# The experts' scatter adds its rows inside the transfer instead of gathering and adding them first

## The chip, the cores and the metric

The kernel runs on one core of a Trainium2 chip. The metric is the device time of one execution in microseconds (us), lower is better. TensorE (PE) does the matrix products, its weight loads are a row of their own (PEld), VectorE (DVE) and ScalarE (ACT) do the elementwise work, GpSimd (POOL) does small elementwise work and issues every indirect transfer, that is every transfer whose rows are picked by a list of indices. SyncE (SP) issues plain transfers. All transfers run on the core's 16 DMA engines.

## The reference

The block takes `x` of 4 x 2048 tokens with 256 features. A linear attention layer is added to it, then a mixture of experts. The second half is what matters here:

```
h = _layernorm(x) * (1 + cb) + sb                       # x: after attention
logits = h @ w_router.T ; gates = softmax ; top 2 of 8 experts
keep   = place of the token in its expert < capacity    # capacity 1280
topk_gates = topk_gates * keep / (sum + 1e-6)
hidden = silu(h @ w_gate.T)                             # 256 -> 512, shared
y      = sum over experts e: combine[:, e] * (hidden @ w_down[e].T)
x      = x + gb * y
```

A token goes to two experts, so a row of the output receives up to two additions, from two different experts; within one expert a token stands once at most.

## The kernel before, in words

The first stage runs over 16 groups of 512 tokens: attention, router, and the place of each token in its experts' lists. It writes the rows after attention to the output in DRAM (`out`, line 779). With an indirect transfer from POOL (line 641) it also writes one row of 1036 numbers per kept (token, expert) pair to a table of slots in DRAM, 1280 slots per expert: the normalised token, its scale, shift and gate vectors, its eight combine weights and its token number.

The second stage runs over the 8 experts, one after another (`expert`, line 667). An expert has 1280 slots, that is ten tiles of 128 rows. They are worked in three blocks of 4, 4 and 2 tiles (`BLOCKS`); a tile is called by its place j in its block. For each block:

- SP loads the slot rows (`rows`, line 661; four buffers in all, loaded one expert ahead). DVE casts the token numbers to integers (`tok`, line 672) and applies scale and shift (`hm`, lines 688 and 689).
- PE turns `hm` over (line 694), ACT copies it out (`hT`, line 695), PE multiplies by the gate weights (`ph`, line 700), ACT and DVE make the SiLU (`th`, line 708, and `hid`, line 709).
- PE multiplies by the expert's own weights into PSUM (`pe`, line 714; two buffers), eight matmuls per tile. DVE evacuates each tile with the combine weight and the gate into `y` (line 721). The `y` tile holds a block of four tiles and has two buffers, so the first evacuation of a block may start only when the transfers that read the block two before have landed.

The addition to the output takes three steps. At the head of an expert, POOL gathers the output's rows of its ten tiles into `xc` (line 675), ten indirect transfers. DVE adds them (line 725) behind each evacuation. POOL writes the sums back (line 726, called a put below), ten indirect transfers. The same row may have been written by an earlier expert. Therefore every gather waits until all puts of the expert before have landed (`after(got, added)`). `xc` has two buffers by the parity of the expert. In the program the first put of an expert also waits until its gathers have landed.

The instructions of one engine run in the order in which they stand in its queue. In the second stage that order is set by a scheduler that works from the dependencies, not written out by hand. POOL's queue in this stage holds nothing but gathers and puts: ten gathers of expert e, then its ten puts, then the ten gathers of expert e + 1. DVE's queue mixes evacuations, additions, `hid`, `tok` and `hm`, the last two of the next expert's blocks.

Of the kernel before, what the change touches and what calls it, by code (L numbers as in the profile page):

```python
# [36 lines left out]
F32 = mybir.dt.float32  # L37
AF = mybir.ActivationFunctionType
ALU = mybir.AluOpType
AX = mybir.AxisListType  # L40

P = 128
NB, L, D = 4, 2048, 256
# [3 lines left out]
N = NB * L  # L47
# [14 lines left out]
TPE = CAP // P  # L62
# [4 lines left out]
def adaln_block(ctx: ExitStack, tc, x, wqkvT, woutT, wrT, wgT, wdT, cT, wmod, out):  # L67
    nc = tc.nc
# [7 lines left out]
    def bank(name):  # L76
        return ps.tile([P, 512], F32, tag="bank", name=name)
# [5 lines left out]
    def load_x(g):  # L83
# [17 lines left out]
        out=hsel, in_=hsel, compare_op=ALU.is_ge, fill=0.0, base=0,  # L101
# [3 lines left out]
        out=hsel, in_=hsel, compare_op=ALU.is_ge, fill=0.0, base=DH - 1,  # L105
# [3 lines left out]
    for q in range(2):  # L109
# [4 lines left out]
        out=tri8, in_=tri8, compare_op=ALU.is_gt, fill=0.0, base=0,  # L114
# [8 lines left out]
    for j in range(NT):  # L123
        for s in (1, -1):
            nc.gpsimd.affine_select(
                out=spread[:, j], in_=spread[:, j], compare_op=ALU.is_ge, fill=0.0, base=-32 * j * s,
# [111 lines left out]
    def after(later, earlier):  # L238

        for e in earlier:  # L240
            tc.add_manual_dep(
                later.ins, e.ins.name, mybir.DependencyInfo(mybir.DependencyClass.Sync, mybir.DependencyReason.DATA),
                reason="rows in DRAM",
            )

    def apart(inst, group, join=True):

        tc.declare_no_dep(inst.ins, group=group, query=mybir.DependencyQuery.ANY_SYNC, reason="different rows")
        if join:
            tc.add_to_no_dep_group(group, inst.ins)  # L250
# [258 lines left out]
    to_slots, added = [], []  # L509
# [144 lines left out]
    def load_rows(e):  # L654
        wds[e] = e3.tile([P, NF, D], F32, tag="wd", name=f"wd_{e}", bufs=3)
        nc.scalar.dma_start(wds[e], wdT[:, e * D : (e + 1) * D].rearrange("(f p) d -> p f d", p=P))
        rows[e] = []
        for i, n in BLOCKS:
            r = e3.tile([P, 4, W], F32, tag="rows", name=f"rows_{e}_{i}")
            at = e * CAP + i * P  # L660
            load = nc.sync.dma_start(
                r[:, :n, :], slots[at : at + n * P, :].rearrange("(j p) w -> p j w", p=P)
            )
            after(load, to_slots)
            rows[e].append(r)

    def expert(e):
        xc = xcs[e % 2]
        toks = []
        for (i, n), r in zip(BLOCKS, rows[e]):  # L670
            tok = e6.tile([P, 4], I32, tag="tok", name=f"tok_{e}_{i}")
            nc.vector.tensor_copy(tok[:, :n], r[:, :n, O_TOK])
            toks.append(tok)
            for j in range(n):
                got = nc.gpsimd.indirect_dma_start(  # L675
                    out=xc[:, i + j, :],
                    out_offset=None,
                    in_=out[:, :],
                    in_offset=bass.IndirectOffsetOnAxis(ap=tok[:, j : j + 1], axis=0),
                    bounds_check=N - 1,  # L680
                    oob_is_err=False,
                )
                after(got, added)
        added.clear()
        for (i, n), r, tok in zip(BLOCKS, rows.pop(e), toks):
            m = n * P
            hm = e2.tile([P, 4, D], F32, tag="hm", name=f"hm_{e}_{i}")
            nc.vector.tensor_tensor(hm[:, :n], r[:, :n, :D], r[:, :n, O_CB : O_CB + D], ALU.mult)
            nc.vector.tensor_tensor(hm[:, :n], hm[:, :n], r[:, :n, O_SB : O_SB + D], ALU.add)
            hT = e2.tile([P, NH, G], F32, tag="hT", name=f"hTe_{e}_{i}")  # L690
            for h in range(NH):
                pt = bank(f"pte_{e}_{i}_{h}")
                for j in range(n):
                    nc.tensor.transpose(pt[:, j * P : (j + 1) * P], hm[:, j, h * P : (h + 1) * P], ident)  # L694
                nc.scalar.copy(hT[:, h, :m], pt[:, :m])  # L695
            hid = e2.tile([P, NF, G], F32, tag="hid", name=f"hid_{e}_{i}")
            for f in range(NF):
                ph = mbank(f"ph_{e}_{i}_{f}")
                for k in range(NH):
                    nc.tensor.matmul(  # L700
                        ph[:, :m],
                        wg_sb[:, k, f * P : (f + 1) * P],
                        hT[:, k, :m],
                        start=(k == 0),
                        stop=(k == NH - 1),
                    )
                th = e2.tile([P, G], F32, tag="th", name=f"th_{e}_{i}_{f}")
                nc.scalar.activation(th[:, :m], ph[:, :m], AF.Tanh, scale=0.5)  # L708
                nc.vector.scalar_tensor_tensor(hid[:, f, :m], th[:, :m], 1.0, ph[:, :m], ALU.add, ALU.mult)  # L709
            pe = ps_e.tile([P, 4, D], F32, tag="psc", name=f"pe_{e}_{i}")  # L710
            y = e2.tile([P, 4, D], F32, tag="y", name=f"y_{e}_{i}")
            for j in range(n):
                for f in range(NF):
                    nc.tensor.matmul(  # L714
                        pe[:, j, :],
                        hid[:, f, j * P : (j + 1) * P],
                        wds[e][:, f, :],
                        start=(f == 0),
                        stop=(f == NF - 1),
                    )  # L720
                nc.vector.scalar_tensor_tensor(  # L721
                    y[:, j, :], pe[:, j, :], r[:, j, O_CW + e : O_CW + e + 1], r[:, j, O_GB : O_GB + D],
                    ALU.mult, ALU.mult,
                )
                nc.vector.tensor_tensor(y[:, j, :], y[:, j, :], xc[:, i + j, :], ALU.add)  # L725
                put = nc.gpsimd.indirect_dma_start(  # L726
                    out=out[:, :],
                    out_offset=bass.IndirectOffsetOnAxis(ap=tok[:, j : j + 1], axis=0),
                    in_=y[:, j, :],
                    in_offset=None,  # L730
                    bounds_check=N - 1,
                    oob_is_err=False,
                )
                apart(put, f"expert_{e}")
                added.append(put)

# [3 lines left out]
    with tc.manual_schedule(engines={ET.PE, ET.Activation, ET.DVE, ET.Pool}):  # L740
# [26 lines left out]
        for s in range((NG + 2) * NT):  # L767
            g, j = divmod(s, NT)
# [85 lines left out]
    def mbank(name):  # L854
        return ps_m.tile([P, 512], F32, tag="mbank", name=name)

    e2 = ctx.enter_context(tc.tile_pool(name="e2", bufs=2))
    e3 = ctx.enter_context(tc.tile_pool(name="e3", bufs=4))
    e6 = ctx.enter_context(tc.tile_pool(name="e6", bufs=6))
    xcs = []  # L860
    for i in range(2):
        xc = e2.tile([P, TPE, D], F32, tag=f"xc{i}", name=f"xc{i}", bufs=1)
        nc.vector.memset(xc, 0.0)
        xcs.append(xc)
    load_rows(0)
    for e in range(NE):
        if e + 1 < NE:
            load_rows(e + 1)
        expert(e)
# [31 lines left out]
```

## Time and profile before

| | us |
|---|---|
| median of 4 runs (1050.0 to 1059.29) | 1053.91 |
| the profiled execution, its own time | 1063.31 |
| its span in the trace | 1061.6 |
| slot rows of the last group begin to be sent (POOL) | 694.4 |
| first PE work of the experts' stage | 716.2 |
| last put issued (POOL) | 1053.5 |

| engine | busy over the span | share |
|---|---|---|
| PE | 901.4 | 85% |
| DVE | 639.8 | 60% |
| POOL | 566.6 | 53% |
| ACT | 439.9 | 41% |

The profile is of one execution. An engine's busy time is the time of its instructions; "idle before" a line is time in which it stood before that instruction, and the arrow names what came last before it could start. "Landing" of a transfer is the time from its issue to its completion. The granted clock of PE is 1.00 at full speed.

The two groups of indirect transfers that the change touches have 80 instructions each: gathers 84.9 us of POOL's time (1061 ns each on the mean), puts 83.9 us (1049 ns). The 80 additions on DVE take 424 ns each at the median.

### The profile page before, as it was taken

Reading aid. Unit: us, or ns where it says so; the run is one execution under the profiler, and the core shown is the slowest. Engines: PE = TensorE matmul, PEld = TensorE weight load, DVE = VectorE, ACT = ScalarE, POOL = GpSimd, SP = SyncE. Lnnn points to the kernel's source line nnn. Section 1 sums busy time; section 2 is a strip of 40 time slices with the busy share of each in tenths; the row PEclk is TensorE's granted clock in tenths of the full one; section 3 lists DMA queues with packets and bytes.
Section 4 is the critical chain, followed back from the end, with each engine's and each line's share of the span. In section 5 each row is a group of like instructions: output and inputs, shape, how many; then the busy total and the mean of one; then the engine's idle time right before and its main releaser. Section 6 shows DMA issues by size and latency. Waiting matters only on the chain. (4 is left out here: it accounts for less than half of the span.)

```text
span 1061.6 us, 18137 instructions
## 1 busy us (share of the span) xinstructions
PE 901.4 (85%) x6832; PEld 638.0 (60%) x6832; DVE 639.8 (60%) x1244; ACT 439.9 (41%) x1054; POOL 566.6 (53%) x738
## 2 busy tenths in 40 slices
PE   5659998699989999898999988409999898898996
PEld 5437666466656666766666666305676665666664
DVE  3326666558767876876787687435565454454543
ACT  0456665366556656655665533202212212122221
POOL 3023526456667665766756766635355454544653
PEclk9879999799999999999999999659999999999998
DMA  5088988642343344223312111336646645556431
GB/s 198 3 318 325 386 312 294 227 182 104 118 181 128 114 181 181 106 81 124 129 46 89 48 37 45 88 144 240 221 164 211 227 172 194 194 183 226 155 110 55
DMA packets 71096, 173.61 MB, mean 164 GB/s; under 512 B 13664, under 2 KB 34400, under 8 KB 71008
## 3 DMA queue, kind: packets, MB, share of 16 engines
q1 hardware_dynamic: 39040, 101.66, 26.6%
q0 software_dynamic: 26112, 63.45, 16.2%
q10 hardware_dynamic: 5856, 7.35, 2.1%
q8 instruction: 53, 0.87, 0.3%
q14 instruction: 35, 0.29, 0.1%
HBM read 68.66 MB, written 129.20 MB: 186 GB/s over the span
## 5 line engine op out<-in xcount | busy, mean ns | idle before, releaser
L714 PE MATMUL pe<-wd,hid 128*128 128x256 f32 x640 | 164.5, 397 | 21.5 <-DVE y L721 19.5
L436 DVE TENSOR_TENSOR at<-psc,tri 128x1024 f32<-128x1024 f32 x128 | 150.1, 1214 | 22.9 <-PE psc L430 22.9
L641 POOL DMA_INDIRECT slots<-hrow,idx x128 | 130.0, 1016 | 62.2 <-issue 35.3
L714 PEld LDWEIGHTS pe<-wd,hid 128*128 128x128 f32 x640 | 120.2, 195 | 70.8 <-DVE y L721 40.9
L700 PE MATMUL ph<-hTe,wg_sb 128*128 128x512 f32 (+1 forms) x384 | 155.8, 532 | 0.0
L726 POOL DMA_INDIRECT out_dram<-y,tok x80 | 83.9, 1049 | 109.9 <-DVE y L725 60.6
L708 ACT ACTIVATE th<-ph 128x512 f32<-128x512 f32 (+1 forms) x96 | 50.5, 526 | 197.4 <-PE ph L700 192.1
L675 POOL DMA_INDIRECT xc<-out_dram,tok x80 | 84.9, 1061 | 71.4 <-issue 42.9
L700 PEld LDWEIGHTS ph<-hTe,wg_sb 128*128 128x128 f32 x384 | 71.7, 194 | 41.7 <-issue 31.4
L721 DVE SCALAR_TENSOR_TENSOR y<-pe,rows 128x256 f32<-128x256 f32 x80 | 38.6, 483 | 92.8 <-PE pe L714 74.2
L709 DVE SCALAR_TENSOR_TENSOR hid<-th,ph 128x512 f32<-128x512 f32 (+1 forms) x96 | 57.2, 596 | 50.8 <-ACT th L708 50.8
L504 PE MATMUL pw<-wob,oT 128*128 128x256 f32 x256 | 70.7, 400 | 18.1 <-ACT kk L371 14.4
L461 POOL TENSOR_TENSOR s_acc<-s_acc,s_add 128x256 f32<-128x256 f32 x56 | 40.7, 726 | 76.7 <-ACT s_add L460 69.3
L430 PE MATMUL psc<-qeo,k 32*128 32x256 f32 x1024 | 74.2, 404 | 2.2 <-DVE at L436 2.1
L338 DVE SCALAR_TENSOR_TENSOR k<-exk,k 128x512 f32<-128x512 f32 x32 | 23.6, 738 | 85.6 <-ACT k L337 85.6
L504 PEld LDWEIGHTS pw<-wob,oT 128*128 128x128 f32 x256 | 46.6, 193 | 41.0 <-issue 16.6
L483 PE MATMUL po<-at,vpad 128*32 128x128 f32 x2048 | 69.9, 278 | 0.0
L332 PE MATMUL pk<-hTa,wqkv_sb 128*128 128x512 f32 x128 | 63.6, 623 | 4.4 <-ACT k L337 4.4
L332 PE MATMUL pq<-hTa,wqkv_sb 128*128 128x512 f32 x128 | 61.3, 604 | 5.1 <-ACT q L337 5.1
L483 PEld LDWEIGHTS po<-at,vpad 128*32 128x32 f32 x2048 | 52.6, 110 | 21.4 <-issue 21.2
L346 PE MATMUL pv<-wqkv_sb,hTa 128*128 128x256 f32 x256 | 61.9, 397 | 3.6 <-ACT pos L589 3.6
L695 ACT COPY hTe<-pte 128x512 f32<-128x512 f32 (+1 forms) x48 | 24.2, 516 | 86.2 <-PE pte L694 86.0
(153 smaller groups left out, 1667.4 us busy)
## 6 DMA issues: line engine op xcount, KB each, us to landing
slots<-free SPq DMA_DIRECT2D x80, 518.0 KB, 6.9
rows<-slots SPq DMA_DIRECT2D x16, 2072.0 KB, 8.6
rows<-slots SPq DMA_DIRECT2D x8, 1036.0 KB, 5.6
x<-in_x_dram SPq DMA_DIRECT2D x16, 512.0 KB, 4.1
out_dram<-x SPq DMA_DIRECT2D x16, 512.0 KB, 3.2
wd<-in_wdT_dram ACTq DMA_DIRECT2D x8, 512.0 KB, 3.7
slots<-hrow,idx POOLq DMA_INDIRECT x128, 3.4
wmod_sb<-in_wmod_dram ACTq DMA_DIRECT2D x1, 1536.0 KB, 8.7
```

What stands on the lines that cost most here:

```text
L332: nc.tensor.matmul(pq, wqkv_sb[:, k, o + h * P : o + (h + 1) * P], hT[:, k, :], start=(k == 0), stop=(k == NH - 1))
L346: nc.tensor.matmul(pv[:, i * D : (i + 1) * D], hT[:, k, (j + i) * P : (j + i + 1) * P], wqkv_sb[:, k, 2 * D : 3 * D], start=(k == 0), stop ...
L430: nc.tensor.matmul(psc[:, a, h], kT[r : r + 32, h, cols], qeo[r : r + 32, h, :, cols], start=True, stop=True,)
L436: masked = nc.vector.tensor_tensor(at, psc[:, 2 * m : 2 * m + 2].rearrange("p i h q t -> p (i h q) t"), tri.unsqueeze(1).to_broadcast([P, ...
L483: nc.tensor.matmul(po[32 * a : 32 * a + 32, h * P : (h + 1) * P], vp[:, j, h * 4 + a, q : q + 2, :], att[a // 2][:, a % 2, h, q, :], start ...
L504: nc.tensor.matmul(pw[:, :D], oT[:, h, :], wob[:, h, :], start=(h == 0), stop=(h == NH - 1))
L641: row = nc.gpsimd.indirect_dma_start(out=slots[:, :], out_offset=bass.IndirectOffsetOnAxis(ap=idx[:, c, j : j + 1], axis=0), in_=hr[:, j, ...
L675: got = nc.gpsimd.indirect_dma_start(out=xc[:, i + j, :], out_offset=None, in_=out[:, :], in_offset=bass.IndirectOffsetOnAxis(ap=tok[:, j ...
L700: nc.tensor.matmul(ph[:, :m], wg_sb[:, k, f * P : (f + 1) * P], hT[:, k, :m], start=(k == 0), stop=(k == NH - 1),)
L709: nc.vector.scalar_tensor_tensor(hid[:, f, :m], th[:, :m], 1.0, ph[:, :m], ALU.add, ALU.mult)
L714: nc.tensor.matmul(pe[:, j, :], hid[:, f, j * P : (j + 1) * P], wds[e][:, f, :], start=(f == 0), stop=(f == NF - 1),)
L726: put = nc.gpsimd.indirect_dma_start(out=out[:, :], out_offset=bass.IndirectOffsetOnAxis(ap=tok[:, j : j + 1], axis=0), in_=y[:, j, :], in ...
```

## The change

The gathers and the additions go. The put carries an addition (`compute_op=ALU.add`), so that the transfer adds `y` to what stands in the output's row. The wait moves with it: every put of an expert now waits until all puts of the expert before have landed (`prior`). The two `xc` buffers and their clearing go as well. In the changed kernel the put stands on line 715, the evacuation on 711, the product into `pe` on 704.

```diff
     def expert(e):
-        xc = xcs[e % 2]
         toks = []
         for (i, n), r in zip(BLOCKS, rows[e]):
             tok = e6.tile([P, 4], I32, tag="tok", name=f"tok_{e}_{i}")
             nc.vector.tensor_copy(tok[:, :n], r[:, :n, O_TOK])
             toks.append(tok)
-            for j in range(n):
-                got = nc.gpsimd.indirect_dma_start(
-                    out=xc[:, i + j, :],
-                    out_offset=None,
-                    in_=out[:, :],
-                    in_offset=bass.IndirectOffsetOnAxis(ap=tok[:, j : j + 1], axis=0),
-                    bounds_check=N - 1,
-                    oob_is_err=False,
-                )
-                after(got, added)
+        prior = list(added)
         added.clear()
...
-                nc.vector.tensor_tensor(y[:, j, :], y[:, j, :], xc[:, i + j, :], ALU.add)
                 put = nc.gpsimd.indirect_dma_start(
                     out=out[:, :],
                     out_offset=bass.IndirectOffsetOnAxis(ap=tok[:, j : j + 1], axis=0),
...
                     oob_is_err=False,
+                    compute_op=ALU.add,
                 )
+                after(put, prior)
                 apart(put, f"expert_{e}")
                 added.append(put)
...
-    xcs = []
-    for i in range(2):
-        xc = e2.tile([P, TPE, D], F32, tag=f"xc{i}", name=f"xc{i}", bufs=1)
-        nc.vector.memset(xc, 0.0)
-        xcs.append(xc)
     load_rows(0)
```

## The prediction, made before the changed kernel had run

> **What bounds the kernel now.** The groups of instructions come first. The change touches 80 gathers (L675), 80 puts (L726) and 80 additions on DVE. What it can give is limited by the engine that sets the stage's length, so the line of that engine is to be read beside them:
>
> ```profile
> L714 PE MATMUL pe<-wd,hid 128*128 128x256 f32 x640 | 164.5, 397 | 21.5 <-DVE y L721 19.5
> L726 POOL DMA_INDIRECT out_dram<-y,tok x80 | 83.9, 1049 | 109.9 <-DVE y L725 60.6
> L675 POOL DMA_INDIRECT xc<-out_dram,tok x80 | 84.9, 1061 | 71.4 <-issue 42.9
> ```
>
> POOL is free half of the time in this stage, and the time it spends on gathers costs nothing by itself. PE, however, sat idle 19.5 us until an evacuation (L721) had been done. Next I cut the experts' stage at each expert's last evacuation and read PE there. Columns: stretch, its length, busy PE, PEld, DVE, ACT, POOL, then the granted clock, the share of the DMA engines, GB/s.
>
> ```profile
> 757.50:799.00 41.50, 39.35 (x149) 26.61 (x148) 21.86 (x41) 9.29 (x18) 20.29 (x20) 0.96 0.59 206
> 799.00:842.70 43.70, 39.59 (x149) 26.73 (x148) 21.67 (x42) 9.20 (x18) 21.95 (x20) 0.96 0.57 197
> 842.70:886.90 44.20, 39.90 (x150) 26.84 (x150) 21.61 (x41) 9.20 (x18) 21.66 (x20) 0.96 0.56 192
> 886.90:931.00 44.10, 39.59 (x149) 26.91 (x148) 21.71 (x41) 9.20 (x18) 20.97 (x20) 0.96 0.56 192
> 931.00:972.70 41.70, 38.38 (x151) 26.19 (x150) 21.68 (x41) 9.20 (x18) 20.98 (x20) 0.99 0.57 200
> 972.70:1015.80 43.10, 40.77 (x153) 27.46 (x152) 21.72 (x41) 9.89 (x19) 21.38 (x20) 0.96 0.54 184
> ```
>
> Six experts take 258.3 us. PE is busy 237.6 of them and idle 20.7. One expert is 38.4 us of PE work where the clock is nearly full (fifth row), the others take 39.4 to 40.8 us for the same matmuls at a lower clock. PE is the bound. What can be won is its idle time and the time that its clock loses behind it: at most 258.3 - 6 x 38.4 = 27.9 us. DVE (21.7 of 43 us) and POOL (21) are far from being bounds.
>
> Who causes the idle time, from the waits in the experts' stage (us in total, times, longest):
>
> ```profile
> DVE y L721 <- DMA out_dram<-y,tok: 18.6, 4, 5.0
> DVE tok L672 <- DMA rows<-slots: 16.4, 14, 3.7
> DVE y L725 <- DMA xc<-out_dram,tok: 2.6, 1, 2.6
> ```
>
> Four times an evacuation waited for puts to land, and once an addition waited for its gather. The timeline of expert 3 shows one of the four:
>
> ```profile
> 871.82 1.04 POOL L726 DMA_INDIRECT out_dram<-y,tok  x1 [6.15 <-DVE hid L709]
> ...
> 876.25 0.98 POOL L726 DMA_INDIRECT out_dram<-y,tok  x1 [0.31 <-issue]
> ...
> 882.89 0.48 DVE L721 SCALAR_TENSOR_TENSOR y<-pe,rows 128x256 f32<-128x256 f32 x1 [4.72 <-DMA out_dram<-y,tok]
> ...
> 883.43 3.44 PE L714 MATMUL pe<-wd,hid 128*128 128x256 f32 x8 [3.75 <-DVE y L721]
> ```
>
> The chain behind it: the last put of expert 2 is issued at 844.4. The first gather of expert 3 waits for its landing until 851.8, ten gathers at 1.3 us last until 865.6, they land, and only then (871.8) does the first put start, though its row block was evacuated from 855.4 to 863.2. The four puts of that block go out in a burst and land only at 882.8, 6.6 us after the last was issued, because SP starts a 2 MB row load at 876.55. The third block needs that `y` buffer, so its evacuation starts at 882.89, and PE stands for 3.75 us. The eight matmuls that follow take 3.44 us where others take 1.99; the clock says why:
>
> ```profile
> 879.00:883.40 4.40, 0.68 (x7) 0.44 (x5) 0.48 (x1) 0.59 (x1) 2.76 (x3) 1.00 0.88 335
> 883.40:886.00 2.60, 2.57 (x7) 2.08 (x8) 0.50 (x2) 0.00 (x0) 0.98 (x1) 0.58 0.15 54
> 886.00:888.00 2.00, 2.00 (x7) 1.25 (x6) 1.09 (x3) 0.59 (x1) 0.00 (x0) 0.69 0.02 5
> 888.00:890.00 2.00, 2.00 (x8) 1.04 (x7) 0.96 (x3) 0.00 (x0) 1.18 (x1) 1.00 1.00 330
> ```
>
> A stall is paid for twice: 2.60 x 0.42 + 2.00 x 0.31 = 1.7 us more go to the lowered clock.
>
> **The change part by part.** *Gathers off POOL.* Ten instructions of about 1.3 us with their gaps leave each expert, and so does the wait for their landing. A put may now follow its evacuation. In expert 3 the last landing of expert 2 was there at 851.8, and the first block is evacuated from 855.4, so the new wait on all earlier puts has about 4 us of slack. Four puts paced by the evacuations (2.6 us apart) are issued by 865, and land by 872 even with the 6.6 us of the burst; PE wants the buffer at about 878.5. The four stalls go: 3.67 (at 839.2) + 3.75 + 4.01 (927.7) + 3.31 (970.7) = 14.7 us. With the first three goes the lowered clock: the second as above; around 839 0.56 over 2.9 us and 0.79 over 2.0; around 928 0.60 over 2.9 and 0.78 over 2.5: 1.7 us each, 5.1 in all. After the fourth the clock stayed at 1.00.
>
> *Additions off DVE.* 80 x 0.42 us are hidden, DVE being half idle, but one of them held DVE 2.59 us for its gather, and PE stood 2.14 us at 988.39 behind it, with the clock at 0.77 for 3.0 us and 0.80 for 5.0 (1.7 us). Together 3.8 us. At the end the last addition and the step to it go off the path: 0.5 us. Smaller waits of PE on `y` (0.2 to 0.4 us, eight of them, 2.0 in all) may shrink; I count them only in the range. The two clearings of `xc` (2.2 us each) lie in DVE's wait for the first rows: nothing.
>
> *What stays.* PE's and DVE's order is that of before, without the additions; only in the last expert do a few PE instructions change places. The first stage is untouched. DVE's waits for rows (16.4 us, once 1.96 us of PE) stay. Each row load starts when an evacuation frees its buffer, lands after a median of 8.5 us, and is wanted about 9 us later. This is late next: if all six experts lost 2 us of PE there, it would take back 12.
>
> *The added work in a put.* No row of this trace shows a transfer that adds. Its issue on POOL: from 0.98 us (the fastest put) to 2.04 (the slowest). Ten at 2.04 + 0.30 are 23 us of an expert's 39, hidden by PE at both ends; I take 1.05, the mean put. Its time on the DMA engines: queue q0 carried 63.45 MB in 16.2% of 1061.6 us, that is 172 us, so one put of 131 KB takes 0.36 us. Below: 0.36, nothing added. Above: an engine has eight of the 128 rows, and were each to be read, added and written before the next, at the fastest landing of any transfer of this kind (2.4 us), a put would take 19 us. The nearest row is a gather and a put at full rate, 0.71, which replaces the two that ran before; I take it, at no cost. Its landing: 2.8 us as now (below), or 5.7, gather and put in sequence (above); I take 1.5 us more. In mid-stage the slack hides it; at the end it is on the path.
>
> The Trainium skill has a rule against the change: in "Collectives: The Full Stack", section "The bandwidth ceiling: the fold count and why AG ≠ RS ≠ AR", a transfer that adds needs two source reads on one ring and ran at about half the rate of a copy (32.35 against 62.28 GB/s). Worked from that, an estimate, a put would take 0.69 us and the sum would stay. No row here shows it. "DMA: Bandwidth & Descriptors", section "Two DMAs through the same engine are not ordered", saw a second read-modify-write read stale data directly behind the first, but not with five packets between; several are then in flight, which speaks against the 19 us.
>
> *Sum*, against the profiled execution: -14.7 - 5.1 - 3.8 - 0.5 + 1.5 = -22.6, so 1063.3 becomes about 1041. The median of the runs lies 9.4 us lower (0.9%), which no row explains; I take the same saving from it: 1053.9 - 22.6 = **1031**. As a check: six experts at 38.4 of work and 0.6 of remaining waits are 234, against 258.3: 24.3.
>
> **The rivals.** *Faster (the forecast), own range 1022 to 1045.* Low end: no longer landing (1.5), the small waits and the row stall gone (2.0 and 2.0), some 3 of scatter. High end: landing 1.4 more and row stalls of 12. A denser PE might be granted the 0.95 of the attention stage instead of 0.99: 230 us x 4% = 9.7 us, within it.
>
> *No gain: the new wait takes the old one's place, about 1050.* An adding put that lands late holds the next expert's first put. With a landing of L beside the row load, the fourth put of expert 3's first block lands at about 844.4 + 1 + L + 5.2 + L. At L = 14 that meets 878.5, where PE wants the buffer; at L = 16 it is the 882.8 of now, and only the gather's stall (3.8) is saved. For it: the last put of an expert already takes 7.4 us to land. Against it: the addition would have to double that.
>
> *Slower: the adding transfers become the bound.* An expert has ten puts in 39 us. From 3.9 us per put on, wherever it is serial (an engine's rows, or POOL's issue), PE waits for puts. At a quarter of the serial end, four rows in flight, a put takes 4.8 us: 80 x 4.8 = 384 against the 324 that the stage takes from its first evacuation, +60, **1114**. At the full 19.2 us it is 1536, +1212. For it: nothing in the trace bounds it lower. Against it: gathers and puts moved rows at 0.36 us. That the change does not do what it says ends here too: POOL's queue has the same 80 puts and nothing in place of the addition, so an addition not done by the DMA engines would show as a longer POOL instruction.
>
> **How the numbers follow.** Forecast 0.60, no gain 0.10, transfer-bound 0.30, of which 0.14 up to 1115. The range 1022 to 1115 leaves out the 0.16 above. Within 1% (10.5 us, about what a measurement here can tell from no change) lie the second case and the slow end of the first: faster 0.58, same 0.12, slower 0.30.
>
> **What would show it.** Right: DVE's wait for puts near 0, PE busy over 97% of 760 to 1000, expert to expert 39 us, clock near 0.99, POOL below 14 us per expert. Wrong: L715 above 2 us, puts landing after 14 us or more, PE waiting on L711, or rows still later.

## The result, and the profile after

The changed kernel takes 1058.68 us (median of 52 runs, 1053.87 to 1067.3). The kernel before, measured beside it, takes 1057.2 us (78 runs, 1048.14 to 1064.82). The ratio is 1.0021, with a 95% interval of 1.0009 to 1.0033: **no gain**, where 22.6 us were forecast. The profiled execution of the changed kernel took 1054.97 us, its span is 1053.2.

Look at the touched groups first (engine, operation, count; busy us, mean ns of one; idle time ahead of it, and what ended it):

```profile
L704 PE MATMUL pe<-wd,hid 128*128 128x256 f32 x640 | 159.2, 387 | 18.7 <-DVE hid L699 11.5
L715 POOL DMA_INDIRECT out_dram<-y,tok x80 | 130.5, 1631 | 213.6 <-DVE y L711 184.2
```

The gathers and the additions are gone, and a put's issue on POOL has grown from 1049 to 1631 ns. POOL can afford that: it stands 184.2 us waiting for evacuations. On PE the idle time ahead of the expert's products has changed its cause. Before, an evacuation ended 19.5 us of it. Now it is `hid`, 11.5 us. The waits of DVE and then of PE in the experts' stage (us in total, times, longest) say what is behind it:

```profile
DVE y L711 <- PE pe L704: 73.0, 60, 2.2
DVE hid L699 <- ACT th L698: 64.9, 73, 2.1
DVE tok L671 <- DMA rows<-slots: 49.4, 22, 5.1
```

```profile
PE pe L704 <- DVE hid L699: 11.5, 5, 3.4
PE pe L704 <- DVE y L711: 7.2, 13, 1.0
```

No evacuation waits for a put any more (18.6 us before). But the casts of token numbers now wait 49.4 us for slot rows (16.4 before), and PE waits behind them. The timeline of one of the five stalls shows how a cast can stop PE:

```profile
842.17 0.36 SPq L661 DMA_DIRECT2D rows<-slots  x1
...
853.42 0.17 DVE L671 CAST tok<-rows 128x4 int32<-128x4 f32 x1 [5.09 <-DMA rows<-slots]
853.50 0.68 DVE L699 SCALAR_TENSOR_TENSOR hid<-th,ph 128x512 f32<-128x512 f32 x1
854.24 1.22 PE L704 MATMUL pe<-wd,hid 128*128 128x256 f32 x2 [3.39 <-DVE hid L699]
```

The 2 MB row load starts at 842.17, when the last evacuation of an expert frees its buffer (a stretch below ends there, at 841.70). It lands 11.2 us later, and at 853.42 the cast that needs it starts. This cast belongs to the first block of the next expert. DVE's queue has that cast ahead of a `hid` of the running expert, so this `hid` waits though its own inputs are there, and PE stands 3.39 us. Six loads start at an expert's end in this way. The four in the middle landed after 11.3, 11.2, 10.3 and 10.6 us here (started at 799.0, 842.2, 884.4 and 925.8), and after 8.7, 9.1, 8.9 and 8.6 us in the trace of before. The first (11.2 against 11.0) and the last (8.8 against 8.1) differ little.

The six stretches from last evacuation to last evacuation (columns as before: length; busy PE, PEld, DVE, ACT, POOL; clock, DMA share, GB/s):

```profile
757.20:798.50 41.30, 38.03 (x150) 25.80 (x149) 18.00 (x32) 9.30 (x18) 16.21 (x10) 1.00 0.67 179
798.50:841.70 43.20, 39.44 (x153) 26.35 (x152) 18.08 (x33) 9.79 (x19) 16.74 (x10) 1.00 0.66 170
841.70:883.90 42.20, 38.45 (x147) 26.23 (x146) 17.97 (x33) 8.62 (x17) 16.41 (x10) 0.96 0.62 168
883.90:925.30 41.40, 38.65 (x150) 25.93 (x150) 17.84 (x32) 9.37 (x19) 16.41 (x10) 1.00 0.66 173
925.30:966.60 41.30, 38.21 (x150) 25.64 (x148) 17.91 (x33) 9.34 (x19) 16.44 (x10) 1.00 0.67 173
966.60:1007.60 41.00, 40.06 (x155) 27.04 (x154) 18.57 (x33) 10.17 (x20) 16.41 (x10) 1.00 0.67 165
```

They sum to 250.4 us, PE busy in 232.8 (before: 258.3 and 237.6). The clock is back, as forecast, except after the one long stall. PE's idle time is 17.6 us, hardly less than the 20.7 of before. And the DMA engines are busier (0.62 to 0.67 against 0.54 to 0.59) while they move less (165 to 179 GB/s against 184 to 206).

### The profile page after: what moved, and what is told of

It is laid out like the page before. It is cut to its first block, busy times and chain, and to the rows that moved or that the text cites. A ratio compares the mean times of both kernels' runs of the same rounds, so it can differ in the third digit from the quotient of the medians.

```text
span 1053.2 us, 17781 instructions
## 1 busy us (share of the span) xinstructions
PE 894.4 (85%) x6832; PEld 633.0 (60%) x6832; DVE 603.6 (57%) x1162; ACT 439.6 (42%) x1054; POOL 528.2 (50%) x658
## 3 DMA queue, kind: packets, MB, share of 16 engines
q1 hardware_dynamic: 39040, 101.66, 26.9%
q0 software_dynamic: 29952, 52.96, 18.6%
## 5 line engine op out<-in xcount | busy, mean ns | idle before, releaser
L715 POOL DMA_INDIRECT out_dram<-y,tok x80 | 130.5, 1631 | 213.6 <-DVE y L711 184.2
L704 PE MATMUL pe<-wd,hid 128*128 128x256 f32 x640 | 159.2, 387 | 18.7 <-DVE hid L699 11.5
L704 PEld LDWEIGHTS pe<-wd,hid 128*128 128x128 f32 x640 | 116.5, 190 | 65.4 <-DVE y L711 26.0
L346 PEld LDWEIGHTS pv<-wqkv_sb,hTa 128*128 128x128 f32 x256 | 48.6, 194 | 11.9 <-ACT pos L589 5.0
L430 PEld LDWEIGHTS psc<-qeo,k 32*128 32x128 f32 x1024 | 46.4, 184 | 14.7 <-PE pq L332 2.5
```

The source lines that it names most:

```text
L346: nc.tensor.matmul(pv[:, i * D : (i + 1) * D], hT[:, k, (j + i) * P : (j + i + 1) * P], wqkv_sb[:, k, 2 * D : 3 * D], start=(k == 0), stop ...
L430: nc.tensor.matmul(psc[:, a, h], kT[r : r + 32, h, cols], qeo[r : r + 32, h, :, cols], start=True, stop=True,)
L704: nc.tensor.matmul(pe[:, j, :], hid[:, f, j * P : (j + 1) * P], wds[e][:, f, :], start=(f == 0), stop=(f == NF - 1),)
L715: put = nc.gpsimd.indirect_dma_start(out=out[:, :], out_offset=bass.IndirectOffsetOnAxis(ap=tok[:, j : j + 1], axis=0), in_=y[:, j, :], in ...
```

## The experiments

Two theories stood at the start. **A**: the puts' stalls were real and are gone, but the row loads are now late, because the adding transfer holds the DMA engines; more row buffers or a plain transfer bring the gain back. **B**: the stalls of the traced execution were never what the median pays, and the change gives little with or without the addition. The first group of runs shared one chip, on which before took 1057.7 us (17 runs). The two later groups ran on two other chips, each about 4% slower, nearly all of it ahead of the experts' stage (the first evacuation at 769.6 and 772.2 instead of 728.6 us in the changed kernel's traces). Each kernel is compared with before on its own chip.

**Before, traced a second time** (no edit).

> The kernel before, unchanged, a second profiled execution. Theory A (the stalls are real, the row loads took the gain back): DVE's wait for puts again near 18 us in three or four places of 4 to 5 us, each followed by a clock of 0.6 to 0.8, and a stage of about 323 us from the first evacuation to the last. Theory B (the traced execution was a slow one; a usual one has smaller stalls, so there was little to gain): a span of 1050 to 1056, DVE's wait for puts below 10 us, and a stage below 318 us.

Measured: 1058.04 us; from first to last evacuation 320.4 us, 323.4 in the first trace. The waits of DVE in this trace, and then two of the stalls on PE in its timeline:

```profile
DVE tok L672 <- DMA rows<-slots: 24.2, 14, 4.7
DVE y L721 <- DMA out_dram<-y,tok: 9.1, 2, 4.7
```

```profile
807.30 1.22 PE L714 MATMUL pe<-wd,hid 128*128 128x256 f32 x2 [3.06 <-DVE hid L709]
...
920.48 3.78 PE L714 MATMUL pe<-wd,hid 128*128 128x256 f32 x8 [3.76 <-DVE y L721]
```

The same program shows two put stalls instead of four, and more waits for rows: the casts for the next expert's first block wait 4.69, 1.69 and 2.99 us (at 806.41, 848.35 and 889.54), but only 0.35 us and nothing behind the two put stalls. The reading is that the kernel pays for late puts **or** for late rows, since a stall by a put draws the row loads apart. The first trace does not show it as clearly (the same casts wait 1.44 us with no put stall ahead, then 1.65, 1.34, 0.98 and 0.20 behind the four); the third `y` buffer below does. So both theories are half right: the first trace's four put stalls are not what every execution pays, but each execution pays something.

**Six row buffers in the changed kernel.** A load can then start earlier: that of an expert's first block at 815.73 us, 18.4 us ahead of the last evacuation of the expert two before, where in the changed kernel it starts 0.5 us behind it. The scheduler also orders this build differently: 32 of PE's 1184 and 44 of DVE's 248 instructions of the stage stand elsewhere in their queues.

```diff
-            r = e3.tile([P, 4, W], F32, tag="rows", name=f"rows_{e}_{i}")
+            r = e3.tile([P, 4, W], F32, tag="rows", name=f"rows_{e}_{i}", bufs=6)
```

> The changed kernel with six row buffers in place of four, so that a row load starts one or two blocks earlier. Theory A: DVE's wait for rows falls from 70 us to below 30, PE's wait on hid (11.5 us) goes, the stage falls from 315 to 303-308 us, and the kernel is 8 to 13 us (0.8 to 1.2%) faster than the kernel before. Theory B: rows were not what cost the time; within 0.4% of the kernel before.

Measured: 1040.6 us (1038.56 to 1045.01, 6 runs), ratio 0.9858 (0.9818 to 0.9898). Its stretches:

```profile
755.90:795.10 39.20, 37.37 (x150) 25.86 (x149) 18.03 (x31) 9.20 (x18) 16.40 (x10) 1.00 0.68 183
795.10:834.10 39.00, 37.50 (x151) 26.00 (x149) 18.07 (x32) 9.20 (x18) 16.40 (x10) 1.00 0.69 186
834.10:872.80 38.70, 37.41 (x150) 25.91 (x149) 18.07 (x31) 9.20 (x18) 16.40 (x10) 1.00 0.69 182
872.80:911.90 39.10, 37.53 (x152) 26.02 (x150) 18.11 (x32) 9.20 (x18) 16.40 (x10) 1.00 0.68 185
911.90:951.10 39.20, 37.40 (x150) 25.89 (x149) 18.12 (x31) 9.20 (x18) 16.43 (x10) 1.00 0.68 183
951.10:989.60 38.50, 38.06 (x151) 25.93 (x150) 18.12 (x31) 9.30 (x18) 17.39 (x10) 1.00 0.44 92
```

The 39 us per expert that the prediction had as its sign are there, with the addition in the transfer, the same puts and the same landing waits. The gain, 17.1 us by medians, is above the 8 to 13 expected. What is different is when a row load may start, and the order of those instructions; no run separates the two. Casts still wait for rows (25.8 us), but PE stands behind `hid` in six pieces of 1.8 us at most, 8.4 us in all. The DMA share, 0.68, is as high as in the changed kernel, so it is not the DMA engines' throughput that bounds.

**The addition left out of the transfer** (the `compute_op` line removed).

> The changed kernel with plain puts: nothing is added, each put overwrites the output's row, so the sum with the row after attention and with the other expert is left out. Everything else, waits too, is as in the changed kernel. It prices the addition in the transfer. Theory A: a put issues in 1.0 us instead of 1.55, its transfers take 0.36 us of the DMA engines instead of about 1, row loads at an expert's end land 2 us sooner, PE's wait on hid falls from 11.5 us to below 4, and the kernel is 7 to 12 us faster than the kernel before. Theory B: within 0.4% of the kernel before, as the changed kernel is.

Measured: 1043.15 us (1042.15 to 1048.96, 6 runs), ratio 0.9873 (0.9834 to 0.9912). Its put group, then its waits for rows on DVE:

```profile
L715 POOL DMA_INDIRECT out_dram<-y,tok x80 | 84.6, 1057 | 251.8 <-DVE y L711 220.1 <-DMA rows<-slots 28.2 <-DMA out_dram<-y,tok 1.9
```

```profile
DVE tok L671 <- DMA rows<-slots: 37.9, 18, 4.4
```

One operand of one instruction is the only difference (PE, DVE and ACT run the same order), and it is worth 1.0021 - 0.9873 = 1.48% of 1057.7, **15.7 us** (the changed kernel's ratio is over all of its runs; by the ends of plain's interval 11 to 20; I had expected plain puts to be 7 to 12 us faster than before, and by medians they are 14.6). The queues say what the operand does. First the indirect transfers' queue of the changed kernel, then that of the plain one (packets, MB, share of 16 engines):

```profile
q0 software_dynamic: 29952, 52.96, 18.6%
```

```profile
q0 software_dynamic: 22272, 52.96, 13.2%
```

The same bytes take 7680 more packets. That is 96 more per put: 128 packets of 1 KB, one per row, where a plain put can go in 32 of 4 KB. Their time is 18.6% of 1053.2 = 195.9 us against 13.2% of 1046.4 = 138.1, so 0.72 us more for each of 80 puts. A put's landing goes from 3.0 to 4.4 us at the median of those puts whose landing the profile gives (40 and 30 of 80). The row loads (all 24, median) land after 9.1 us instead of 8.3, though the queue that carries them needs the same time for its packets (26.9% of 1053.2 is 283, 27.0% of 1046.4 is 283).

Is the late row load the addition's doing alone? No. A load of 1 MB and one of 2 MB follow each other at the end of an expert, and how far apart they start counts too. Where they start 5.2 us apart in all three kernels (the second at 799.52 before, 797.21 plain, 799.00 changed), the second lands after 8.7, 9.1 and 11.3 us. But in the second trace of before a load with the same distance (at 794.40) lands after 12.0 us, with plain puts, so this one place does not show the addition at work. After the next three experts the put stalls of before had drawn the two 11 us apart, and the second landed after 8.6 to 9.1. Without those stalls they start 5.8 to 6.8 us apart, and it lands after 10.6 to 11.0 us with plain puts, 10.3 to 11.2 with adding ones. Over the four traces with plain puts and four row buffers (before twice, third `y` buffer, plain), loads 11 us apart land after 8.3 to 9.1 us and loads 5 to 7 us apart after 8.4 to 12.0. So a removed stall tends to make the loads later, with either kind of put; how much later the addition makes a single load isn't shown.

The two traces show only part of the 15.7 us. PE's waits behind `hid` and evacuations are 9.1 and 2.9 us with plain puts, 11.5 and 7.2 with adding ones, 6.7 more in all (I had expected the 9.1 to be below 4); the traced execution of the plain kernel (1048.96) was the longest of its six.

**A third `y` buffer in the kernel before.** This takes the put stalls away and nothing else; the order of PE, DVE and ACT stays.

```diff
-            y = e2.tile([P, 4, D], F32, tag="y", name=f"y_{e}_{i}")
+            y = e2.tile([P, 4, D], F32, tag="y", name=f"y_{e}_{i}", bufs=3)
```

> The kernel before with three y buffers in place of two; gathers, additions and waits as before. The third block of an expert no longer needs the buffer of its first block. Theory A: DVE's wait for puts falls from 18.6 us to about 0, and the kernel is 10 to 20 us (1 to 2%) faster than the kernel before. Theory B: the wait falls but a usual execution had little of it; less than 6 us faster.

Measured: 1053.41 us (1049.78 to 1057.58, 12 runs), ratio 0.9964 (0.9939 to 0.9988). DVE's and PE's waits:

```profile
DVE tok L672 <- DMA rows<-slots: 36.9, 18, 4.6
```

```profile
PE pe L714 <- DVE y L721: 7.5, 8, 2.9
PE pe L714 <- DVE hid L709: 6.2, 3, 2.6
```

No evacuation waits for a put here, and the gain is 4.3 us, not the 14.7 plus clock of the prediction: the wait for rows rises from 16.4 or 24.2 us to 36.9. This is the changed kernel's trade in the old kernel, without its transfer. I had written down 10 to 20 us, or less than 6 if a usual execution had little of the stalls.

**The row buffers in the same space.** `rows` gets three buffers for blocks of 4 tiles and two for blocks of 2, sixteen tiles as before. First in the kernel before, then in the changed one, then together with the third `y` buffer; beside them the changed kernel is traced again.

```diff
-            r = e3.tile([P, 4, W], F32, tag="rows", name=f"rows_{e}_{i}")
+            r = e3.tile([P, n, W], F32, tag=f"rows{n}", name=f"rows_{e}_{i}", bufs={4: 3, 2: 2}[n])
```

> The kernel before with the same space for rows, split by the size of a block: three buffers of four tiles and two of two tiles, in place of four of four tiles. The first load of an expert then reuses the buffer of the second block two experts back and starts one block (about 10 us) earlier. Theory 'two stalls hide each other' (an expert of the kernel before is held either by its puts or by its row loads; taking away one lets the other come to light): within 0.5% of the kernel before, with four or more waits of 3 to 5 us for puts. Rival (the row loads alone were the stall that matters): 10 us or more faster.

> The changed kernel with the same split of the row buffers: no more space than it had, but the first load of an expert starts a block earlier. Theory 'two stalls hide each other': with the puts' stall gone by the change, the row loads' stall goes too, DVE's wait for the first rows of an expert falls to near 0, and the kernel is 12 to 18 us (1.1 to 1.7%) faster than the kernel before. Rival (six buffers helped for another reason, such as a deeper prefetch of all blocks): less than half of what six buffers gave, under 8 us.

> The kernel before, gathers and additions kept, with both cures: three y buffers and the split of the row buffers. Theory 'two stalls hide each other': the two cures together give much more than the 4 us of three y buffers alone, 12 to 16 us, so that most of what the changed kernel can reach needs no adding transfer. Rival (the gathers themselves cost something that only the change takes away): under 8 us.

> The changed kernel, unchanged, a second profiled execution. If its first traced execution (315 us from first to last evacuation, its own time 3.7 us below the median) was a lucky one, the second has a stage of 316 to 321 us, with PE waiting behind late row loads 14 us or more instead of 12. In either case DVE's wait for puts is 0.

| kernel | us | ratio to before (1097.9) |
|---|---|---|
| before, rows 3 + 2 | 1086.27 (1081.54 to 1089.26, 6 runs) | 0.9886 (0.9862 to 0.991) |
| before, rows 3 + 2, three `y` | 1086.5 (1086.07 to 1091.56, 5 runs) | 0.9891 (0.9868 to 0.9914) |
| changed, rows 3 + 2 | 1082.7 (1078.28 to 1085.35, 6 runs) | 0.9856 (0.9832 to 0.988) |
| changed, traced again | 1096.93 (1 run) | |

DVE's waits in the kernel before with this one edit:

```profile
DVE tok L672 <- DMA rows<-slots: 14.1, 11, 2.6
DVE y L721 <- DMA out_dram<-y,tok: 5.5, 2, 3.6
```

I had expected that a cure of one stall alone would let the other one out, so that this edit would do nothing in the kernel before. That fell: it is worth 11.6 us, and fewer **put** stalls are left too, 5.5 us against 18.6 and 9.1 in the two traces of before. A third `y` buffer on top adds nothing, where I had written 12 to 16 us for both cures together. A likely reason stands in the prediction's own timeline: the puts of the traced stall landed late when SP had started a row load 0.3 us after the last of them (the 1 MB one of a third block, not 2 MB as the prediction says). One of the two stalls left here is of that kind: a row load starts at 910.96, 0.4 us after the fourth put of its block, and the evacuation at 915.70 waits 3.55 us. That the moved loads cured the others isn't shown, for the scheduler also reordered this build: 77 of PE's 1184 and 52 of DVE's 330 instructions of the stage stand elsewhere (52 and 43 of 248 in the changed kernel's build). So not every microsecond need be the buffers'. The changed kernel with this edit is 15.2 us faster than before, though its casts still wait 16.9 us for rows. The second trace of the unchanged one shows again what it waits for: PE 11.4 us behind `hid`, 314.9 us from first to last evacuation, as in its first trace (I had expected 316 to 321).

**The addition alone.** In the kernel before, the put adds and waits for the earlier puts, and DVE's addition is dropped. The gathers stay, into buffers that nobody reads.

```diff
-                nc.vector.tensor_tensor(y[:, j, :], y[:, j, :], xc[:, i + j, :], ALU.add)
                 put = nc.gpsimd.indirect_dma_start(
...
+                    compute_op=ALU.add,
                 )
+                after(put, prior)
```

> The changed put with the gathers put back: puts add in the transfer, the additions on DVE stay away, but the ten gathers of every expert run as before, with their waits, into xc that nobody reads. It separates the two halves of the change. Theory (an expert pays once, either for its late puts or for its late row loads, and the adding put costs DMA time that makes row loads later): the gathers bring the late puts back, in four or more experts (DVE's wait for puts 15 us or more), and with dearer puts the kernel is 8 to 20 us slower than the kernel before. Rival (the gathers never mattered): as the changed kernel, within 4 us of the kernel before.

Measured: 1122.43 us (1117.39 to 1124.37, 6 runs) against 1095.17, ratio 1.0239 (1.0213 to 1.0266), **27 us slower**. DVE's wait for the puts, then PE's behind it:

```profile
DVE y L722 <- DMA out_dram<-y,tok: 27.4, 5, 6.8
```

```profile
PE pe L715 <- DVE y L722: 31.0, 17, 5.2
```

Here the adding puts do stall the evacuations, more than the plain puts of before did (18.6 and 9.1 us): a gather must wait for the landing of all puts (24.9 us on POOL, 17.6 in the first trace of before), and the longer issues stand in the same queue. So the two parts of the change pull against each other: the addition costs, the missing gathers pay for it. The 27 us lie above the 8 to 20 that I had written down.

**The addition with rows out of the way.** Six row buffers with and without `compute_op`, and the changed kernel as it is, on the same chip.

> The changed kernel with six row buffers and plain puts that overwrite instead of adding (the sum is left out). Against the same kernel with adding puts it prices the addition where no row load is late. Theory (the addition costs only through late row loads): at most 4 us apart, where with four row buffers the two were 15 us apart. Rival (the adding transfers cost time of their own, at the end or on POOL): 8 us or more apart.

> The changed kernel with six row buffers again, on the same chip as the two beside it: 1.2 to 1.6% faster than the kernel before, as on the other chip, and within 4 us of the one with plain puts.

> The changed kernel, unchanged, timed on the same chip as the three beside it: within 0.5% of the kernel before. Its profile: DVE's wait for puts 0, five or six waits of PE behind late row loads of 1.4 to 3.4 us, 41 to 42 us from expert to expert.

| kernel | us | ratio to before (1095.17) |
|---|---|---|
| plain put, six rows | 1077.03 (1076.39 to 1085.3, 5 runs) | 0.9846 (0.9821 to 0.9872) |
| adding put, six rows | 1082.82 (1078.41 to 1086.66, 6 runs) | 0.9896 (0.9867 to 0.9924) |
| adding put, four rows (the change) | 1100.42 (1096.84 to 1106.64, 10 runs) | 1.0051 (1.0029 to 1.0073) |

With six row buffers the addition costs 5.8 us, between the two numbers expected (at most 4, or 8 and more), and the two intervals meet. With four it cost 15.7 on the first chip. Each pair has one order of instructions, so some 10 us of the price go with the six-buffer build, whose rows load earlier. Of the other 5.8, the traces show 4: PE's wait behind `hid` in front of the gate product goes from 3.9 to 7.9 us. Three casts now wait 6.1 us in all for puts to land, since they overwrite the token lists that those puts read; in the plain kernel none does.

## Why the prediction was wrong

**The ledger.** By medians against before on the first chip: the put stalls alone -4.3 (third `y` buffer); gathers and additions gone as well, the sum left out, 1043.15 - 1053.41 = -10.3; the addition in the transfer +15.7. Forecast were -24.1 for all that is removed and +1.5 for the addition. Measured are -14.6 and +15.7. They sum to 1.1 us slower, near the 1.5 of the medians.

**Right: the mechanism of the puts, and of the clock.** "The four stalls go" holds in all three traces of the changed kernel: no evacuation waits for a put, and the slack of the new wait on POOL was there (POOL waited for puts 1.2 us in the first and third trace, 4.3 us in the second). In the first trace the only stretch with a lowered clock is that of the 3.39 us stall.

**The step that failed first: "I take 1.05, the mean put" and "the nearest row is a gather and a put at full rate, 0.71 ..., at no cost".** The amounts were near: 0.36 + 0.72 = 1.08 us of an engine's time per put instead of 0.71, 1.63 us of issue (inside the 0.98 to 2.04 given), 1.4 us more landing (1.5 given). The conclusion "at no cost" was wrong: leaving the addition out of the transfer gives 15.7 us. I had asked whether POOL or the puts' own engine time could become the bound, and neither did. I had not asked who shares the engines with them: the row load, with a slack of about zero. That the cost goes through this load is supported by the six-buffer runs, and in part argued.

The rule that I had weighed against the row, half the rate for a transfer that adds ("Collectives: The Full Stack", section "The bandwidth ceiling: the fold count and why AG ≠ RS ≠ AR"), would give 0.36 x 1.93 = 0.69 us, an estimate. The runs show three times 0.36 for this row-wise scatter, so the measurement decides; the rule pointed the right way, and I turned it into "the sum would stay". The other page, "DMA: Bandwidth & Descriptors", section "Two DMAs through the same engine are not ordered", was used against the serial 19 us per put, and there the trace agrees: a median landing of 4.4 us, 9.1 at most, leaves no room for eight read-modify-writes one after another at 2.4 us each.

**The step that held the answer: "This is late next: if all six experts lost 2 us of PE there, it would take back 12."** It stood in the high end of the range and should have been in the sum. PE lost 11.5 us there in the trace. The row was on the page: a median landing of 8.5 us against a need after 9 leaves almost no slack, and a removed stall brings the loads closer together. Over all loads the median landing is 8.3 us with plain puts and 9.1 with adding ones.

**A mis-sized term: "I take the same saving from it".** Four put stalls, 14.7 us and 5.1 of clock, are one execution's price, and that one was long (1063.31 against a median of 1057.2). The second trace has two. And where the puts were not waited for, the rows were (36.9 us with the third `y` buffer), so the saving is not the sum of the stalls: that buffer found 4.3 us, where 14.7 and 5.1 were forecast.

**The rivals.** "No gain, about 1050" came near in size but not by its mechanism: it needed puts that land after 14 to 16 us, and the slowest in the first trace took 9.1. "The adding transfers become the bound", 0.30 of the chance, has nothing for it: at 3.9 us per put and more it was far off. Of the signs, POOL below 14 us per expert failed by the longer issue (16.2 to 16.7), expert to expert 39 us failed, and "rows still later" was the one that came.

**What stays open.** The three traced executions of the changed kernel take 314.9, 314.9 and 313.3 us from first to last evacuation, 6 to 10 less than the two of before (323.4, 320.4). The medians say 1.5 us more. A traced execution of the changed kernel lies 3.6 to 3.7 us below its median in the two cases with a median, those of before lie at theirs or above (1058.04 to 1057.7, 1063.31 to 1057.2). So the usual execution of the changed kernel loses some 4 us that no trace shows, and the plain one's trace is 5.8 above its median, which is why the traces show less than half of the 15.7. That it is more of the same row stalls is likely, since six row buffers remove the loss in the timed runs too, but it isn't shown.

**A version that beats both** is the changed kernel with the row buffers split 3 + 2: 1.4% faster than before, with no more space for rows than before. Six full row buffers give 1.4% and 1.0% on two chips. By the runs at hand the build with these buffers does most of it: it gives the kernel before 1.1% already, and the two intervals overlap.

## What to carry to other kernels

When a stall is removed, list every transfer whose slack that stall had been feeding, with its landing time beside the time at which it is needed; one with no slack takes the gain back, and belongs in the sum, not in the range. Price added DMA work by what shares the engines with it, not by its own queue: here 0.72 us per put, hidden for POOL and for the puts, cost 15.7 us, some 10 of them gone where the row loads of another engine could start earlier. And trace the kernel before twice: stalls that trade places from one execution to the next cannot be added up.

## What the hardware showed that was not expected

- An indirect put that adds goes out row by row: 128 packets of 1 KB instead of 32 of 4 KB, 1.55 us of issue on POOL at the median instead of 0.98, and about three times the engine time (1.08 instead of 0.36 us for 131 KB).
- The clock does not go by the length of a stall alone. After the 3.39 us stall the granted clock was 0.50 for 1.8 us and 0.69 for 2.0, while after one of 2.33 us (at 811.17) the stretch shows 1.00. In the first trace of before, stalls of 1.96 us (at 769.79) and 2.14 us (at 988.39) were followed by a lower clock (0.50 from 771.18 to 774.59 and from 989.63 to 993.04), and the one of 3.31 us (at 970.69) was not. The Trainium skill ("TensorE: Matmul & The Clock Gate", section "Part 1: The HAM clock gate (the "warmup" mystery)") has the clock halved after an idle window of about 3.4 us; the 3.39 us stall is near that, the 1.96 and 2.14 us ones are well below it.
- Cutting the same sixteen tiles of row buffer to the blocks' sizes gave the kernel before 11.6 us, in a build that the scheduler also ordered anew. In the ring of four equal buffers a block of 2 tiles holds a buffer for 4, and an expert's first load waits for the last block of the expert two before.
